# A graph network on one core: feed-forward products in groups of two node blocks, with all up products of a pair in one slot and both down products in the next

## The chip, the cores and the metric

The kernel runs on one core of one Trainium2 chip. The metric is device time in microseconds of one launch, smaller is better. The engines are named as in the profile: PE is TensorE (matmuls, with PEld its weight loads), DVE is VectorE, ACT is ScalarE, POOL is GpSimd and SP is SyncE. L12 is line 12 of the kernel.

## What is computed

A two-layer graph network on 10,000 nodes of 512 features and 160,000 edges that are sorted by target node. All data is fp32. Cut to what matters:

```python
# layer 0
h  = relu(layernorm(x))
ha = h @ rel_W[0..3] + rel_b              # four products per node
agg = segment_sum(ha[src, edge_type], dst) / max(deg, 1)
x1 = layer_norm(h + h @ self_W + self_b + agg, ln1_w, ln1_b)
f  = gelu(x1 @ W1 + b1) @ W2 + b2         # W1: 512 x 1024, W2: 1024 x 512
x  = x + layer_norm(x1 + f, ln2_w, ln2_b)
# layer 1: two SAGE layers on relu(layernorm(x))
h  = relu(layernorm(x))
for W_self, W_neigh, b in (...):
    h = relu(h @ W_self + segment_mean(h[src], dst) @ W_neigh + b)
x  = x + h
```

The change touches only the line that computes `f`, the feed-forward part of layer 0, and what is queued around it.

## The kernel before

The nodes are cut into 79 blocks of 128 (the last, number 78, has 16 nodes and is taken first). The program has three stages. Stage 1 (0 to 1611 us of the profiled execution) normalizes x and makes the five products of each block; beside it the edge lists are prepared. Stage 2 (1611 to 3616 us) does, for each block, the gather and sum of layer 0, both layer norms and the feed-forward part, and writes `xn`, the new x, and `h1`, the input of layer 1. The rest (3616 to 7341 us) is two SAGE layers over the same blocks. Only stage 2 is changed. The order of the instructions on each engine is that of the code, written out by hand; tiles come from pools with a given number of buffers, and an instruction that writes a buffer waits until the buffer's last readers are done.

**Gather and sums.** For a block, `gather` (L649) issues indirect DMAs on POOL, each bringing 128 rows of 2 KB into a row buffer. There is a ring of 28 such buffers (`RING`, L640). Each block has 5 "others", whose rows are summed over edges by one-hot matmuls, and 11 "mine" gathers, which are added on DVE (`add`, L688). Each 4th block adds a gather for a "tail" that is shared by 4 blocks, each 16th one that is shared by 16; tails have two buffers of their own. POOL issues in the order tails, others, mine. `sums` (L674) makes 7 matmuls on PE into a PSUM tile `pa`: first the two tails, then the others.

**The loop over blocks** (L903 to L932) is written as one slot for each block b. A slot holds, in this order: the load of `xs` for the block after next (SP, 512 KB for each pair of blocks); the one-hot tile of block b+1 (DVE); `second`, which adds the finished down products of the slot before to `rest` and takes their statistics (DVE); the adds of block b (11 on DVE), one scaling and statistics; then one part of the queued products on PE, but for its last call; then `finish` (a Sqrt on ACT over all statistics of the slot) and `scaled`; then the last call of the part; and last `begin` for block b+1, which is its gather on POOL and its sums on PE.

`scaled` (L848) applies norms on ACT: the first norm of block b, then the last norm of the blocks whose down products were two slots back (`h1`, stored by SP), then the second norm of those of the slot before. DVE then makes `rest` (what is added to the feed-forward result, 11 buffers) and the new `xr`, and SP stores `xn`.

**Groups.** Blocks are taken in groups of 4 (`plan`, L880): block 78 alone, then 19 groups of 4, then one of 2. A `Group` holds `x1T`, the transposed normalized block columns (two buffers, 512 columns wide), and `hid`, the hidden layer, transposed, 8 tiles of 128 x 512 (one buffer). `turn` makes 4 PE transposes and 4 ACT copies for one block; it is called in the middle of the slot after the block's own. `up(f)` makes 4 matmuls with up to 512 columns into `ph` (two PSUM buffers) and one Gelu on ACT into `hid`. `down(b)` loads `xr` (SP, for each pair of blocks) and makes 8 matmuls into `po` (two PSUM buffers). An fp32 matmul is two records in the trace.

`parts` (L791) cuts a group into four parts: ups 0 to 3, ups 4 to 7, the downs of its first two blocks, the downs of its last two. The parts of a group are put in the queue in the first slot of the next group, after that slot has taken its part; so they are taken one per slot from the slot after. Over a quad of slots, ups fall on the blocks with b%4 = 1 and 2 and downs on those with b%4 = 3 and 0. After the last block a closing loop (L935) takes what is left, one part in each pass, without gathers.

`Sqrt` and `Gelu` are in different activation tables; each change between them is a table load on ACT (L778, L821).

Of the kernel before, what the change touches and what calls it, by code (L numbers as in the profile page):

```python
# [8 lines left out]
F32 = mybir.dt.float32  # L9
# [7 lines left out]
P = 128  # L17
# [4 lines left out]
def kernel(  # L22
# [34 lines left out]
    N, D = x.shape  # L57
# [3 lines left out]
    KC = D // P  # L61
    FC = F // P
# [69 lines left out]
    def rows_of(t, g):  # L132

        b, nb, r = g
        return t[b * P:b * P + nb * r, :].rearrange("(c p) d -> p c d", p=r)
# [500 lines left out]
    def aligned(ctxa):  # L636
# [4 lines left out]
        rest = list(range(full))  # L641
        blocks = ([full] if N % P else []) + rest

        def height(b):
            return min(P, N - b * P)
# [49 lines left out]
        with ExitStack() as s:  # L695
            wp = s.enter_context(tc.tile_pool(name="wp2", bufs=1))
            gp = s.enter_context(tc.tile_pool(name="gp", bufs=1))
            sp = s.enter_context(tc.tile_pool(name="sp", bufs=3))
            psT = s.enter_context(tc.tile_pool(name="psT2", bufs=2, space=PSUM))
            psH = s.enter_context(tc.tile_pool(name="psH", bufs=2, space=PSUM))  # L700
# [8 lines left out]
            def pair(t, b, n, name, bufs):  # L709

                return (gp.tile([P, 2, D], F32, name=name, bufs=bufs)[:height(b), :n],
                        rows_of(t, (b, n, height(b))))
# [10 lines left out]
            def load_res(b, n):  # L723
                v, at = pair(xr_d, b, n, "xr", 3)
                nc.sync.dma_start(v, at)
                for c in range(n):
                    xrs[b + c] = v[:, c, :]
                xrs[b, n] = v
# [22 lines left out]
            class Group:  # L751


                def __init__(self, bs):
                    self.bs, self.r = bs, height(bs[0])
                    self.xT = gp.tile([P, KC, 4 * P], F32, name="x1T", bufs=2)
                    self.hid = None

                def turn(self, b, v):
# [10 lines left out]
                def up(self, f):  # L770
                    n = len(self.bs) * self.r
                    if self.hid is None:
                        self.hid = gp.tile([P, FC, 4 * P], F32, name="hid")
                    ph = psH.tile([P, 4 * P], F32, name="ph")
                    for k in range(KC):
                        nc.tensor.matmul(ph[:, :n], w1s[:, k, f * P:(f + 1) * P],  # L776
                                         self.xT[:, k, :n], start=(k == 0), stop=(k == KC - 1))
                    nc.scalar.activation(self.hid[:, f, :n], ph[:, :n], AF.Gelu,  # L778
                                         bias=b1s[:, f:f + 1], scale=1.0)

                def down(self, b):
                    c, r = self.bs.index(b), self.r
                    if c % 2 == 0:
                        load_res(b, min(2, len(self.bs) - c))
                    po = psO.tile([P, D], F32, name="po")
                    for f in range(FC):
                        nc.tensor.matmul(po[:r], self.hid[:, f, c * r:(c + 1) * r], w2s[:, f, :],  # L787
                                         start=(f == 0), stop=(f == FC - 1))
                    return b, po

                def parts(self):  # L791

                    ups = [lambda f=f: self.up(f) for f in range(FC)]
                    downs = [lambda b=b: self.down(b) for b in self.bs]
                    return [ups[:FC // 2], ups[FC // 2:]] + [downs[i:i + 2]
                                                             for i in range(0, len(downs), 2)]

            COLS = 8

# [32 lines left out]
            rests = {}  # L832
# [15 lines left out]
            def scaled(got, first):  # L848

                nonlocal third, now  # L850
                if first:
                    b, c = first
                    r, v = height(b), nodes[b]
                    now.apply(v[:r], v[:r], c, r, AF.Identity)
                if third:
                    h1, at = pair(h1_d, third[0][0], len(third), "h1", 2)
                    for k, (b, c) in enumerate(third):
                        now.apply(h1[:, k, :], xrs.pop(b), c, height(b), AF.Relu)
                    nc.sync.dma_start(at, h1)
                third = []  # L860
                for b, v, c in got:
                    r = height(b)
                    now.apply(v[:r], v[:r], c, r, AF.Identity)
                if first:
                    b, c = first
                    r, v = height(b), nodes[b]
                    rests[b] = gp.tile([P, D], F32, name="rest", bufs=11)
                    nc.vector.tensor_tensor(rests[b][:r], v[:r], ln1w[:r], op=OP.mult)
                    nc.vector.tensor_tensor(rests[b][:r], rests[b][:r], lnb2[:r], op=OP.add)
                now = Scales()  # L870
                for b, v, c in got:
                    r = height(b)
                    nc.vector.tensor_tensor(v[:r], v[:r], ln2w[:r], op=OP.mult)
                    nc.vector.tensor_tensor(xrs[b], xrs[b], v[:r], op=OP.add)
                    third.append((b, now.stats(xrs[b], r)))
                if got:
                    b, n = got[0][0], len(got)
                    nc.sync.dma_start(rows_of(xn_d, (b, n, height(b))), xrs.pop((b, n)))

            plan = [[b] for b in blocks[:len(blocks) - len(rest)]]  # L880
            plan += [rest[:-2][i:i + 4] for i in range(0, len(rest) - 2, 4)] + [rest[-2:]]
            queue = []
            turning = None
            held = begin(blocks[0], hots(blocks[0]), table)
# [18 lines left out]
            i = 0  # L903
            grp = None
            for bs in plan:
                for b in bs:
                    r = height(b)
                    if b == bs[0]:
                        before, grp = grp, Group(bs)
                    if i + 2 < len(blocks):  # L910
                        load(blocks[i + 2])
                    if i + 1 < len(blocks):
                        hot = hots(blocks[i + 1])
                    got = second()
                    pa, mine = held
                    add(b, pa, mine)
                    v = nodes[b]
                    nc.vector.scalar_tensor_tensor(v[:r], pa[:r], rdeg[:r, b:b + 1], v[:r],
                                                   op0=OP.mult, op1=OP.add)
                    first = (b, now.stats(v[:r], r))  # L920
                    part = products(queue.pop(0) if queue else [], turning)
                    next(part)
                    now.finish()
                    scaled(got, first)
                    next(part, None)
                    if i + 1 < len(blocks):
                        held = begin(blocks[i + 1], hot, table)

                    if b == bs[0] and before:
                        queue += before.parts()  # L930
                    turning = lambda g=grp, b=b, v=v: g.turn(b, v)
                    i += 1  # L932
            turning()
            queue += grp.parts()
            while queue or fed or third:  # L935
                got = second()
                part = products(queue.pop(0) if queue else [], None)
                next(part)
                now.finish()
                scaled(got, None)  # L940
                next(part, None)
# [6 lines left out]
        for step, (h_d, ws, wn, bs) in enumerate(((h1_d, ws1, wn1, bs1), (h2_d, ws2, wn2, bs2))):  # L948
            with ExitStack() as s:
# [54 lines left out]
                for i, b in enumerate(blocks):  # L1004
                    r = height(b)
                    q, c = place[b]
# [295 lines left out]
    with tc.If(go > 0) as cmp:  # L1302
        with ExitStack() as ctxa:
            with tc.manual_schedule():
                aligned(ctxa)
# [31 lines left out]
```

## Time and profile before

| | |
|---|---|
| three runs | 7339.11, 7335.75, 7313.08 us; median 7335.75 |
| profiled execution | 7342.91 us, of which the span of its instructions is 7341.1 |
| granted PE clock, mean | 0.881 |
| PE busy, whole span | 5665.5 us (77%) |
| DVE, POOL, ACT busy | 3658.8, 3792.5, 1016.3 us |
| stage 2, 1611 to 3616 us | PE 1700.0, DVE 1233.8, POOL 1248.4, ACT 583.1 us busy |
| DMA in stage 2 | 210 GB/s, the 16 DMA engines busy 69% |

How to read the lines below. A line of the timeline gives start and length in us, the engine, the line of the kernel, the operation, the tile written and the tiles read, shapes and how many equal instructions in a row it stands for; in brackets is the idle time of the engine just before, and what ended it. "issue" is a wait that the profile doesn't explain, "remote" one that ended with a signal whose sender it doesn't know. A view of stretches gives the busy time of each engine in a window, with the number of its instructions, then the granted PE clock as a share of full speed, the share of the DMA engines and GB/s.

### The profile page before, as it was taken

What the parts mean: (1) busy time and instruction counts of PE and PEld (TensorE: products, weight loads), DVE (VectorE), ACT (ScalarE), POOL (GpSimd) and SP (SyncE); (2) the same over time, 40 slices, a digit from 0 to 9 for tenths busy, and PEclk for the clock granted to TensorE, in tenths of its full rate; (3) what the DMA queues carried; (4) which work ended last, traced back from release to release, by engine and by line L of the source; (5) the groups of instructions that cost most, each with busy time, mean ns of one, the idle gap of its engine ahead of it and who ended that gap; (6) DMA issues with size and microseconds to landing.
All of it is one profiled execution on the core that took longest, in us unless ns stands there. A gap on an engine that the chain in (4) does not pass through costs nothing.

```text
span 7341.1 us, 49909 instructions
## 1 busy us (share of the span) xinstructions
PE 5665.5 (77%) x14251; PEld 2553.8 (35%) x14251; DVE 3658.8 (50%) x7297; ACT 1016.3 (14%) x1667; POOL 3792.5 (52%) x3927
## 2 busy tenths in 40 slices
PE   6999999986889889899766666766665666666666
PEld 3444444432334334344323332332322333332232
DVE  5347777424666666666334434443333444443444
ACT  1000000002232233233201100110100000000000
POOL 0000000016666666666266666666656666666665
PEclk9999999997999999999878888888887888888888
DMA  3222222236767777777366666666666777777775
GB/s 141 109 97 98 93 104 92 85 135 194 211 205 224 224 221 225 220 227 225 129 198 206 206 209 204 208 204 206 203 196 208 220 216 216 219 217 214 220 219 169
DMA packets 456992, 1361.46 MB, mean 185 GB/s; under 512 B 71746, under 2 KB 71746, under 8 KB 446578
## 3 DMA queue, kind: packets, MB, share of 16 engines
q0 software_dynamic: 308768, 1008.91, 46.5%
q1 hardware_dynamic: 134034, 262.10, 10.1%
q10 hardware_dynamic: 13904, 87.17, 3.0%
q8 instruction: 114, 1.87, 0.1%
q14 instruction: 172, 1.41, 0.1%
HBM read 1150.89 MB, written 207.01 MB: 185 GB/s over the span
## 4 chain that ended last, share of the span: by engine, by line
PE 39%; issue 20%; another core or an unknown queue 17%; ACT 3%; DVE 3%; DMA 1%; POOL 1%; ACTq 0%; POOLq 0%; DVEq 0%; SPq 0%
PE pa L680 11%; PE ph L776 6%; PE pm L613 6%; PE po L787 6%; PE po L984 4%; PE po L1018 4%; DVE pa L692 2%; PE pT L167 1%; POOL rows L653 1%; ACT hTb L168 1%; ACT mTb L168 1%; ACT mb L1014 0%; PE pT L764 0%; ACT hid L778 0%
## 5 line engine op out<-in xcount | busy, mean ns | idle before, releaser
L692 DVE TENSOR_TENSOR pa<-pa,rows 128x512 f32<-128x512 f32 x2574 | 1798.5, 699 | 1002.9 <-issue 689.3
L653 POOL DMA_INDIRECT rows<-h_d,row x1716 | 1663.6, 969 | 929.1 <-issue 428.5
L984 PE MATMUL po<-wns,mTb 128*128 128x512 f32 (+1 forms) x1264 | 704.5, 709 | 587.5 <-issue 310.2
L680 PE MATMUL pa<-rows,hot 128*128 128x512 f32 (+1 forms) x2358 | 1080.7, 605 | 46.1 <-issue 20.6
L653 POOL DMA_INDIRECT rows<-hall_d,row x858 | 849.8, 990 | 504.4 <-issue 193.7
L613 PE MATMUL pm<-wrel,hT 128*128 128x512 f32 (+1 forms) x2528 | 1098.1, 592 | 0.0
L1018 PE MATMUL po<-wss,hTb 128*128 128x512 f32 (+1 forms) x1264 | 700.6, 706 | 475.6 <-ACT hTb L168 387.3
L653 POOL DMA_INDIRECT rows<-h_d,orow x786 | 754.1, 959 | 400.1 <-issue 220.7
L776 PE MATMUL ph<-x1T,w1s 128*128 128x512 f32 (+2 forms) x1344 | 606.1, 605 | 158.9 <-ACT hid L778 111.4
L613 PEld LDWEIGHTS pm<-wrel,hT 128*128 128x128 f32 (+1 forms) x2528 | 477.0, 189 | 605.8 <-issue 595.3
L680 PEld LDWEIGHTS pa<-rows,hot 128*128 128x128 f32 (+1 forms) x2358 | 454.2, 193 | 641.9 <-issue 603.7
L984 PEld LDWEIGHTS po<-wns,mTb 128*128 128x128 f32 (+1 forms) x1264 | 280.8, 228 | 995.9 <-issue 691.6
L653 POOL DMA_INDIRECT rows<-hall_d,orow x393 | 373.1, 949 | 434.8 <-SPq L1333 308.5
L787 PE MATMUL po<-w2s,hid 128*128 128x512 f32 (+1 forms) x1264 | 561.4, 596 | 23.2 <-issue 20.8
L1018 PEld LDWEIGHTS po<-wss,hTb 128*128 128x128 f32 (+1 forms) x1264 | 273.7, 228 | 846.3 <-ACT hTb L168 440.4
L680 PE MATMUL pa<-tail,hot 128*128 128x512 f32 x936 | 457.7, 607 | 53.3 <-issue 49.2
L990 DVE TENSOR_TENSOR po<-po,bss 128x512 f32<-128x512 f32 (+1 forms) x79 | 55.0, 696 | 811.3 <-remote 702.7
L487 POOL DMA_INDIRECT win<-rec_d,at x79 | 74.8, 947 | 727.9 <-issue 637.1
L776 PEld LDWEIGHTS ph<-x1T,w1s 128*128 128x128 f32 x1344 | 263.8, 204 | 470.7 <-issue 332.1
L616 DVE TENSOR_TENSOR ha<-pm,brel 128x512 f32<-128x512 f32 (+1 forms) x316 | 216.4, 687 | 405.1 <-PE pm L613 405.1
L994 DVE TENSOR_TENSOR ob<-po,bss 128x512 f32<-128x512 f32 (+1 forms) x79 | 54.4, 688 | 597.4 <-remote 268.8
L787 PEld LDWEIGHTS po<-w2s,hid 128*128 128x128 f32 (+1 forms) x1264 | 236.2, 190 | 312.5 <-issue 308.0
(233 smaller groups left out, 4171.5 us busy)
## 6 DMA issues: line engine op xcount, KB each, us to landing
hall_d<-ha ACTq DMA_DIRECT2D x78, 1024.0 KB
hb<-h_d SPq DMA_DIRECT2D x38, 1024.0 KB
rows<-h_d,row POOLq DMA_INDIRECT x1716
xs<-xs_d SPq DMA_DIRECT2D x39, 512.0 KB
xr<-xr_d SPq DMA_DIRECT2D x39, 512.0 KB
xn_d<-xr SPq DMA_DIRECT2D x39, 512.0 KB
h_d<-h SPq DMA_DIRECT2D x39, 512.0 KB
xg<-in_x_dram SPq DMA_DIRECT2D x19, 1024.0 KB
```

The costliest lines, as they stand in the source:

```text
L167: nc.tensor.transpose(p[:, k, :r], rows[:, k * P:(k + 1) * P], ident[:r, :r])
L168: nc.scalar.copy(dest, p[:, :, :r])
L487: nc.gpsimd.indirect_dma_start(out=win[:, c, :], out_offset=None, in_=rec_d, in_offset=bass.IndirectOffsetOnAxis(ap=at[:, c:c + 1], axis=0))
L613: nc.tensor.matmul(pm[:r], hT[:, k, :r], w[:, k, :], start=(k == 0), stop=(k == KC - 1))
L616: nc.vector.tensor_tensor(ha[:r, j - 1, :], pm[:r], brel[:r, (j - 1) * D:j * D], op=OP.add)
L653: nc.gpsimd.indirect_dma_start(out=t[:n], out_offset=None, in_=table, in_offset=bass.IndirectOffsetOnAxis(ap=idx, axis=0))
L680: nc.tensor.matmul(pa[:r], hot[:, t, :r], others[t], start=(t == order[0]), stop=(t == order[-1]))
L692: nc.vector.tensor_tensor(pa[:r], pa[:r], t[:r], op=OP.add)
L776: nc.tensor.matmul(ph[:, :n], w1s[:, k, f * P:(f + 1) * P], self.xT[:, k, :n], start=(k == 0), stop=(k == KC - 1))
L787: nc.tensor.matmul(po[:r], self.hid[:, f, c * r:(c + 1) * r], w2s[:, f, :], start=(f == 0), stop=(f == FC - 1))
L984: nc.tensor.matmul(po[:r], mT[:, k, :r], wns[:, k, :], start=False, stop=(k == KC - 1))
L1018: nc.tensor.matmul(po[:r], hT[:, k, :r], wss[:, k, :], start=(k == 0), stop=False)
```

## The change

Groups have two blocks in place of four. A group has two parts: all eight ups (32 matmuls with 256 columns in place of 512, and 8 Gelus of 256 columns), and both downs. Over the loop, the ups of a pair now fall on blocks with odd b and the downs on those with even b. `x1T`, `hid` and `ph` have half as many columns; `load_res` is called once for each group; `rest` has 8 buffers in place of 11. The calls in a part stand around `finish` and `scaled` as before: with 8 ups, seven come before them and one after, and `turn` is called after the fourth; with 2 downs, one comes before and one after. Counted over the program, Gelus go from 168 to 320, and the table loads from 63 of each table to 80 of each. The matmuls of the downs, the gathers and the DVE adds are the same in number, and so are SP's loads and stores; the order of SP's list is another, with one of `xn`, `xs`, `xr` and `h1` for each pair.

```diff
@@ class Group
-                    self.xT = gp.tile([P, KC, 4 * P], F32, name="x1T", bufs=2)
+                    self.xT = gp.tile([P, KC, 2 * P], F32, name="x1T", bufs=2)
@@ def up(self, f)
-                        self.hid = gp.tile([P, FC, 4 * P], F32, name="hid")
-                    ph = psH.tile([P, 4 * P], F32, name="ph")
+                        self.hid = gp.tile([P, FC, 2 * P], F32, name="hid")
+                    ph = psH.tile([P, 2 * P], F32, name="ph")
@@ def down(self, b)
-                    if c % 2 == 0:
-                        load_res(b, min(2, len(self.bs) - c))
+                    if c == 0:
+                        load_res(b, len(self.bs))
@@ def parts(self)
-                    return [ups[:FC // 2], ups[FC // 2:]] + [downs[i:i + 2]
-                                                             for i in range(0, len(downs), 2)]
+                    return [ups, downs]
@@ def scaled(got, first)
-                    rests[b] = gp.tile([P, D], F32, name="rest", bufs=11)
+                    rests[b] = gp.tile([P, D], F32, name="rest", bufs=8)
@@ plan
-            plan += [rest[:-2][i:i + 4] for i in range(0, len(rest) - 2, 4)] + [rest[-2:]]
+            plan += [rest[i:i + 2] for i in range(0, len(rest), 2)]
```

## The prediction, as recorded before the result

> **What bounds the kernel now.** I read the page's list of engines, then the change's own stretch (stage 2, 1611 to 3616 us), then its waits, then the timelines of PE, ACT, POOL and SP inside single slots. "Slot" means one pass of the loop over blocks: products (one part of a queued group), then the sums of the next block. Busy time by stretch:
>
> ```profile
> core 0: us, PE busy (x) PEld busy (x) DVE busy (x) ACT busy (x) POOL busy (x), PEclk, DMA share, GB/s
> 1650.00:3502.00 1852.00, 1588.75 (x3747) 701.61 (x3747) 1165.44 (x1930) 534.68 (x859) 1220.13 (x1249) 0.92 0.72 217
> 3502.00:3616.00 114.00, 94.58 (x246) 47.85 (x244) 52.26 (x107) 47.02 (x70) 0.00 (x0) 0.92 0.16 56
> ```
>
> PE is busy 86% of the main stretch, ACT 29%. An undisturbed slot is all PE:
>
> ```profile
> 2561.91 7.03 PE L776 MATMUL ph<-x1T,w1s 128*128 128x512 f32 x16
> 2568.78 0.60 PE L764 MATMUL pT<-ident,xs 128*128 128x128 f32 x4
> 2569.22 7.03 PE L776 MATMUL ph<-x1T,w1s 128*128 128x512 f32 x16
> 2576.08 1.88 PE L680 MATMUL pa<-tail,hot 128*128 128x512 f32 x4
> 2577.80 4.46 PE L680 MATMUL pa<-rows,hot 128*128 128x512 f32 x10
> 2582.09 3.60 PE L776 MATMUL ph<-x1T,w1s 128*128 128x512 f32 x8
> ```
>
> From start to start, sums are 6.01 us, half the products 6.87, the transposes 0.44, the other half 6.87: 20.2 us. Taking every slot by the start of its first L680 matmul, 30 of the 68 slots from 1859 to 3502 us last 20.2 us, within 0.2; the mean of the 68 is 24.2. So stage 2 loses 4 us per slot, and the forecast is about where those lie. POOL is close behind: an issue takes 0.95 and a gap of 0.30, 1.25 us, times 16.3 gathers of a block is 20.4 us, and its pauses for the 28 ring buffers add more:
>
> ```profile
> 2560.42 0.94 POOL L653 DMA_INDIRECT rows<-hall_d,row  x1 [2.96 <-PE pa L680]
> 2583.57 1.12 POOL L653 DMA_INDIRECT rows<-hall_d,row  x1 [3.45 <-PE ph L776]
> 2608.31 0.94 POOL L653 DMA_INDIRECT rows<-hall_d,row  x1 [2.58 <-PE po L787]
> ```
>
> So POOL's cycle is some 23.5 us, and neither engine can be sped up alone. The largest losses are four slots of 41.8, 39.2, 45.7 and 39.2 us (at 1858.8, 1987.9, 2154.0 and 2928.4), all with ups. Inside the third, ACT and then PE:
>
> ```profile
> 2180.59 0.69 ACT L778 ACTIVATE hid<-ph,b1s 128x512 f32<-128x512 f32 x1 [18.13 <-issue]
> 2192.52 0.69 ACT L778 ACTIVATE hid<-ph,b1s 128x512 f32<-128x512 f32 x1 [11.24 <-remote]
> ```
>
> ```profile
> 2160.18 7.13 PE L776 MATMUL ph<-x1T,w1s 128*128 128x512 f32 x16
> 2181.33 5.75 PE L776 MATMUL ph<-x1T,w1s 128*128 128x512 f32 x8 [13.58 <-ACT hid L778]
> 2193.26 6.61 PE L776 MATMUL ph<-x1T,w1s 128*128 128x512 f32 x8 [6.17 <-ACT hid L778]
> ```
>
> The first ph was complete near 2164, its gelu began at 2180.59, with ACT idle and the table loaded. PE had two ph buffers, filled both, and stood for 13.6 and 6.2 us. In the slot at 2555.9 the same gelu began at 2565.55, at once. Comparing the end of each ph with the start of its gelu over the stage, the lag is 0.04 us in most cases within 8 us of a POOL pause, and 3.7 to 17 us once POOL has issued for more than 14 us without one. I read this as PE's signals arriving late while gathers run without a break. The trace shows the delay, not its cause.
>
> **What the Trainium skill says.** "TensorE: Matmul & The Clock Gate", Back-to-back issue gap: the gap goes with the free size, plus 2.5 ns. The trace agrees: 128x512 records are 0.43 us apart, the 128x256 ones at the stage's end 0.215 ("3569.68, x16 in 3.62 us"), weight loads hidden. "Perfetto Trace Analysis", Summary: the profiler window per engine type: for TensorE the end is estimated, and the semaphore's propagation is outside the record. The trace agrees: 16 us lie there above. Same page, Optimizing Scalar/DVE Operations: if ACT is not saturated but causes bubbles elsewhere, splitting instructions may complete work sooner. This speaks for the change; no row of before tests it at 256 columns beside gathers. "DMA: Bandwidth & Descriptors", Queues, rings and completion order: each engine alternates between its queues by packets, so a burst on SP's queue slows the gathers; SP issues four 512 KB transfers from 2505.18 to 2507.17, and the core's DMA engines are 99% busy from 2506 to 2522.
>
> **The change, part by part.**
>
> Matmuls. Ups per pair: 8 x 4 with 256 columns, at 2 records of 0.215 us, 13.7 us; before, 4 x 4 at 2 x 0.43, also 13.7. Downs unchanged. A slot's PE work stays 20.2 us, the total too: 0.
>
> ACT. Gelus go from 152 of 0.69 to 304 of 0.47 (the 256-column row at the end), +38 us; table loads for Gelu and for Sqrt, 63 each to 80 each, are 34 more at 1.28, +44 us. ACT has 1300 us idle in the main stretch: 0 on the path by itself. A load delays one gelu, priced with the round trip below. If that cover went, all 82 us would show.
>
> DVE, POOL. The same adds and gathers. Buffers: a rest lives 6 blocks with 8 buffers, as it lived about 9 with 11; x1T has two groups of buffers, hid one, read before its next write in PE's own order. No new wait: 0.
>
> SP. Per pair now xn, xs, xr and h1 leave in separate slots, where before a quad's D1 let off four at once, xr and xs having stood behind a store of h1 that waited for ACT (496 us in 20 waits of SP's queue). After the burst quoted above PE crawled through the next sums (2520.6 to 2536) and POOL paused 5.26 us. Moving the burst may give up to 6 us per quad, 18 x 6 = 108; it may also give nothing, as the crawl also follows from late signals alone. I take 0 and keep the gain for a rival.
>
> Tail. After the last block PE has no gathers beside it. Now it drains six part-slots there: U2, D1, D2 (13.7 each), then the last pair's U1, U2 (6.9 each) and D (13.7) = 68.6 us. After: D, U, D = 41.2. The 27.5 us move into early slots that had no products; the early ones wait for gathers (1610.9 to 1650: PE 16.7 of 39), so there they cost nothing, if block 78's slot does not get worse (now 59.9 us; all eight of its ups now share it). Gain 27.5, between 0 and 33 (the tail's 3.88 and 4.08 us waits included).
>
> The wait that is added. A U slot now makes eight round trips PE, ACT, PE, with two ph buffers each filled in 1.72 us in place of 3.43; so a signal may be 1.7 us late, not 3.4, before PE stands. Behind PE's ups stand the transposes, the rest of the ups, and the next block's sums, and behind those sums stand POOL's ring and DVE's adds. And U slots move: now ups fall on blocks with b%4 = 1 and 2, downs on 3 and 0; after, ups on each odd b, downs on each even. In the pass with b%4 = 3 POOL issues the gathers of a block with tails, which lie in buffers of their own, and I find its pause missing there in most quads: it runs some 40 us without a break (up to 2531.65, then 5.26 us). Now only downs lie there, which need nothing back from ACT; PE runs on and merely crawls. After, eight ups lie there. Bounds: at the least nothing (or a gain, as under SP); at the most, every such slot as long as the four above.
>
> Price: quads (four slots) that hold a starved slot last 102.4, 106.3, 106.2 and 108.9, mean 105.9; the 13 others average 93.8. One starved slot costs 12 us net, for a late PE lets POOL refill. There are 18 quads' worth, 4 starved now. I take two in three afterwards, 12: 8 x 12 = +96. Sum: 96 - 27.5 = +68.5. On the profiled execution (7342.9: span 7341.1 and 1.8 around it) 7411.4; that execution lies 7.2 above the median of 7335.75, so 7404.
>
> **The rivals.**
>
> Every quad starves: 14 x 12 = +168 - 27.5: about 7476. For: half the tolerance, twice the trips. Against: the present ups starve in four slots of 34 only.
>
> The other side, faster. One mechanism: U and D alternating keeps POOL pausing each slot, so no gelu is late, and the burst is gone: the four starved slots go, -48, and the tail, -27.5: 7260; with some of the burst's 108, lower. For: the gelu behind f5 falls due some 11 us after a pause, where about half the lags are still short. Against: lags above 14 us are always long, and the b%4 = 3 pause is missing. It decides at whether POOL pauses in that pass.
>
> Even: three more starved quads, +36 against -27.5: 7344.
>
> The change does what it says; ups and downs are cut in pairs in the text of the loop, and the order is fixed by that text.
>
> **How the numbers follow.** Chances: forecast 0.42, all starve 0.16, even 0.20, faster 0.22. 0.5%, or 37 us, is about what a measurement of this kernel can tell from no change: slower above 7372 has 0.58, same 0.20, faster 0.22. The likeliest sign's own range is 7375 to 7490. The range 7255 to 7490 leaves half of the faster case (0.11) and about half of the worst (0.08) outside.
>
> **What would show it.** Right: in after, slots with b%4 = 3 near 40 us with PE's ph waiting on ACT hid L778 well above its 111 us; tail after the last gather near 85 us, not 114; slots without stalls still 20.2. Wrong: a mean slot under 23 us and ph waits below 111 (then alternation helped), or L776's 256-column records further apart than 0.215 beside gathers (then the bound is PE). An execution whose early slots (to 1900 us) hold the difference would mean that block 78's eight ups decide.

## The result, and the profile after

The kernel after took 7540.45 us (median; 7529.55 to 7575.69) against 7330.53 for the kernel before beside it (7313.08 to 7339.11): 1.03 times the time of before, 95% interval 1.0266 to 1.0334. The forecast was 7404, slower; the range ended at 7490. The profiled execution of after took 7575.69, that of before 7342.91, 232.8 less.

The same stretch of stage 2, from the sums of the first blocks to the last gather (engines' busy time, then PE clock, DMA share, GB/s), is longer by 238 us, with the same work in it:

```profile
core 0: us, PE busy (x) PEld busy (x) DVE busy (x) ACT busy (x) POOL busy (x), PEclk, DMA share, GB/s
1650.00:3740.00 2090.00, 1590.61 (x4868) 947.60 (x4869) 1148.20 (x1914) 615.70 (x1034) 1202.96 (x1229) 0.87 0.61 190
```

PE and POOL are about as busy, in us, as in the 1852 us of before; there is just more idle time. PE's own waits in this stretch, in all, times, longest:

```profile
PE ph L776 <- issue: 292.6, 34, 24.1
PE ph L776 <- ACT hid L778: 206.2, 29, 30.1
PE pa L680 <- DMA rows<-hall_d,orow: 12.2, 1, 12.2
```

Before, the first two came to 39.5 and 107.3. Now 499 us of PE's idle time lie ahead of ups, nothing ahead of downs. A slot is counted as in the prediction, from the sums of a block to those of the next; a U slot runs the ups of a pair, a D slot its downs. D slots take 20.2 us, again and again; of the last 34 U slots, 31 take 32 to 48 us. Averaged over these 68 slots, U slots with b%4 = 1 take 34.0 us, those with b%4 = 3 take 36.2, D slots 20.2 and 20.2. One U slot (PE, ACT, POOL):

```profile
2345.94 1.88 PE L680 MATMUL pa<-tail,hot 128*128 128x512 f32 x4
2347.66 4.46 PE L680 MATMUL pa<-rows,hot 128*128 128x512 f32 x10
2351.95 7.07 PE L776 MATMUL ph<-x1T,w1s 128*128 128x256 f32 x32
2358.86 0.60 PE L764 MATMUL pT<-ident,xs 128*128 128x128 f32 x4
2359.29 3.86 PE L776 MATMUL ph<-x1T,w1s 128*128 128x256 f32 x16
2375.19 5.79 PE L776 MATMUL ph<-x1T,w1s 128*128 128x256 f32 x16 [12.03 <-ACT hid L778]
2380.81 1.88 PE L680 MATMUL pa<-tail,hot 128*128 128x512 f32 x4
```

```profile
2357.33 0.47 ACT L778 ACTIVATE hid<-ph,b1s 128x256 f32<-128x256 f32 x1 [1.25 <-issue]
2360.63 0.47 ACT L778 ACTIVATE hid<-ph,b1s 128x256 f32<-128x256 f32 x1 [2.83 <-PE ph L776]
2364.85 1.50 ACT L766 ACTIVATE x1T<-pT,ln1bc,ln1wc 128x128 f32<-128x128 f32 x4 [3.74 <-remote]
2374.66 0.84 ACT L778 ACTIVATE hid<-ph,b1s 128x256 f32<-128x256 f32 x2 [8.31 <-remote]
```

```profile
2352.06 0.94 POOL L653 DMA_INDIRECT rows<-hall_d,row  x1 [2.22 <-PE pa L680]
...
2370.81 0.95 POOL L653 DMA_INDIRECT rows<-hall_d,row  x1 [0.31 <-issue]
2383.82 1.39 POOL L653 DMA_INDIRECT rows<-hall_d,row  x1 [12.07 <-PE pa L680]
```

The first three Gelus are prompt, the fourth comes 1.6 us late, the copies after it 5.4 us after the transposes' end, and the fifth Gelu 13.5 us after its ph's end (2361.2), 2.9 us after POOL had issued the last gather that it could. The slot's length adds up: sums 6.0, then 19.7 us in which POOL issues 16 gathers (2352.06 to 2371.75), 2.9 until the signals come, 6.15 for the last ups: 34.8, and 34.87 is measured.

"Late" means late after the end that the profile gives for PE's matmuls. These ends are estimated, as the prediction says; whether the product or its signal is late, the trace can't tell.

In this slot PE's granted clock is halved as well, for 13.6 us (columns as in the first view):

```profile
2365.80:2379.40 13.60, 4.21 (x10) 3.41 (x11) 0.00 (x0) 1.78 (x5) 4.73 (x5) 0.50 0.42 127
```

That is not what starts the stall: the fourth Gelu was late at 2360.63 and PE stood from 2363.15. In 32 of the 34 U slots some Gelu or copy comes over 4 us late; in 31 of these the clock is halved in the slot, each time from 3 to 15 us after the first of its late signals had become 0.5 us late. The halved clock costs something afterwards, as the last ups take 5.79 us for 16 records in place of 3.6.

Where the 233 us lie: the start of stage 2 takes 49 us more (the sums of block 5 begin at 1798.0, not 1749.2), the 72 slots after it 240 more (1992.9 for 1752.5), the stretch from the last sums to the SAGE layers 40 less (88.1 for 127.7), the rest 17 less.

### The profile page after: what moved, and what is told of

It reads as the page before. It is cut to its first block, busy times and chain, and to the rows that moved or that the text cites. A ratio compares the mean times of both kernels' runs of the same rounds, so it can differ in the third digit from the quotient of the medians.

```text
span 7573.7 us, 52464 instructions
## 1 busy us (share of the span) xinstructions
PE 5662.2 (75%) x15467; PEld 2813.7 (37%) x15467; DVE 3655.4 (48%) x7295; ACT 1099.7 (15%) x1852; POOL 3796.2 (50%) x3927
## 4 chain that ended last, share of the span: by engine, by line
PE 39%; issue 19%; another core or an unknown queue 19%; ACT 3%; DVE 3%; DMA 1%; POOL 1%; ACTq 0%; POOLq 0%; DVEq 0%; SPq 0%
PE pa L680 10%; PE ph L776 8%; PE po L787 6%; PE pm L613 5%; PE po L983 4%; PE po L1017 4%; DVE pa L692 2%; PE pT L167 1%; DMA rows<-h_d,row 1%; POOL rows L653 1%; ACT hTb L168 1%; ACT x1T L766 1%; ACT mb L1013 0%; ACT mTb L168 0%
## 5 line engine op out<-in xcount | busy, mean ns | idle before, releaser
L680 PE MATMUL pa<-rows,hot 128*128 128x512 f32 (+1 forms) x2358 | 1061.0, 597 | 24.7 <-DMA rows<-hall_d,orow 13.2
L983 PE MATMUL po<-wns,mTb 128*128 128x512 f32 (+1 forms) x1264 | 681.6, 690 | 488.9 <-ACT mTb L168 290.6
L776 PE MATMUL ph<-x1T,w1s 128*128 128x256 f32 (+1 forms) x2560 | 662.7, 419 | 508.6 <-issue 301.8
L776 PEld LDWEIGHTS ph<-x1T,w1s 128*128 128x128 f32 x2560 | 533.1, 215 | 637.1 <-issue 336.0
L680 PE MATMUL pa<-tail,hot 128*128 128x512 f32 x936 | 442.3, 595 | 1.8 <-DVE mv L814 1.8
```

The source lines that it names most:

```text
L680: nc.tensor.matmul(pa[:r], hot[:, t, :r], others[t], start=(t == order[0]), stop=(t == order[-1]))
L776: nc.tensor.matmul(ph[:, :n], w1s[:, k, f * P:(f + 1) * P], self.xT[:, k, :n], start=(k == 0), stop=(k == KC - 1))
L983: nc.tensor.matmul(po[:r], mT[:, k, :r], wns[:, k, :], start=False, stop=(k == KC - 1))
```

## The experiments

The sets were run on different chips, and the chip turned out to matter: on three of them the kernel before takes some 6650 us, on the others 7323 to 7373. Each result is therefore given as a ratio to the kernel before in the same set. Lengths of slots in the first set are compared with the profiles of before and after above, which come from another chip (before: 7330.53 there, 7372.82 here).

Theory A: PE's signals to ACT come late once a certain number of PE instructions has followed the last pause of the gathers. Theory B: the slots starve because the two ph buffers hold half as much PE time as before (the room in ph). Theory A2, formed after the first set: the signals then wait for POOL to stop, and the ring says when.

**First set (before: 7372.82).** e1, the kernel before with narrow ups:

```diff
-                    for k in range(KC):
-                        nc.tensor.matmul(ph[:, :n], w1s[:, k, f * P:(f + 1) * P],
-                                         self.xT[:, k, :n], start=(k == 0), stop=(k == KC - 1))
+                    for c in range(0, n, 2 * P):
+                        m = min(n, c + 2 * P)
+                        for k in range(KC):
+                            nc.tensor.matmul(ph[:, c:m], w1s[:, k, f * P:(f + 1) * P],
+                                             self.xT[:, k, c:m], start=(k == 0),
+                                             stop=(k == KC - 1))
```

> The kernel before (quads), but each up matmul of 512 columns is issued as two of 256; Gelus, parts, buffers and order as before. Theory A (what counts is how many PE instructions follow the last pause of the gathers: signals to ACT come late after some 28 records): the two up slots of a quad, 64 records in place of 32, grow from 20 to 27 us to about 34, downs stay: some 7540 to 7600 us. Theory B (what counts is the room that ph gives, 1.72 us in place of 3.43, and the number of round trips): both are as in the kernel before, so 7335 within 40.

Measured 7460.87, ratio 1.0106 (1.006 to 1.0152), between the two. First up slots of a quad went from 25.8 to 34.5 us in the mean, second ones from 23.6 to 24.2, and the slot of the last two downs from 25.7 to 21.3. Only the ups' matmuls and their weight loads were doubled in number; ph's room and the Gelus are as before. So theory B alone doesn't explain it, and the first up slots starve as theory A says; its second half, that both do, fails. In the timeline of PE the second comes right behind a stall of 23 us, in which POOL too had to stop for 17.5, which may be what spares it.

```profile
3004.47 7.07 PE L778 MATMUL ph<-x1T,w1s 128*128 128x256 f32 x32
3011.38 0.64 PE L764 MATMUL pT<-ident,xs 128*128 128x128 f32 x3
3013.82 0.27 PE L764 MATMUL pT<-ident,xs 128*128 128x128 f32 x1 [1.80 <-issue]
3037.10 9.85 PE L778 MATMUL ph<-x1T,w1s 128*128 128x256 f32 x32 [23.01 <-ACT hid L781]
3046.78 1.88 PE L680 MATMUL pa<-tail,hot 128*128 128x512 f32 x4
```

e2, the kernel after with four ph buffers, two in one tile:

```diff
-                    ph = psH.tile([P, 2 * P], F32, name="ph")
+                    if f % 2 == 0:
+                        self.ph = psH.tile([P, 2, 2 * P], F32, name="ph")
+                    ph = self.ph[:, f % 2, :]
```

> The kernel after, with four ph buffers of 256 columns (two to a bank) in place of two. Theory B: the stall of 12 us in each slot of ups goes, since the first four Gelus are prompt: 7250 to 7330 us. Theory A: PE runs past the ups, but the signals stay late until the gathers pause, so that the downs of the next slot wait for hid, or PE crawls: part of the stall comes back there, 7380 to 7540.

Measured 7714.54, ratio 1.0445 (1.0384 to 1.0507), worse than both theories said. The edit is at fault: a product that goes into one half of a tile waits for the Gelu of the other half (0.56 us with "<-ACT hid L780" or "<-issue", ahead of each pair's second half in the slot at 3201.4). It gave less room, not more, and tells nothing of theory B but that a wait added here costs: U slots took 37.5 and 38.6.

e3, the kernel after with six of a block's eleven "mine" gathers in stage 2 (the first ones are added twice, so this kernel leaves rows out and its sums are others):

```diff
-            return others, [rows(P, row[:, b, t:t + 1]) for t in range(own(b))]
+            mine = [rows(P, row[:, b, t:t + 1])
+                    for t in range(min(6, own(b)) if few else own(b))]
+            return others, (mine * 2)[:own(b)]
```

> The kernel after, in which stage 2 leaves out five of the eleven mine gathers of a block (the first rows are added twice in their place); PE, ACT and DVE work unchanged. If the lateness comes from the unbroken stream of gathers (A): POOL is at 14 us per block, pauses over 5 us in each slot, the Gelus are prompt and slots of ups fall from 36 to 20 to 22 us: 6900 to 7000 us. If it comes from ACT's own chain (table loads, Sqrt, number of Gelus): slots of ups stay at 30 or more, above 7350.

Measured 7145.52, ratio 0.9675 (0.9619 to 0.9731). U slots fell to 26.4 (b%4 = 1) and 20.4 (b%4 = 3), with PE's, DVE's and ACT's work unchanged. So the products and Gelus fit into 20.4 us, and ACT's table loads and Sqrt, which are all still there, don't make the stall by themselves; the stream of gathers is needed for it. The tails say so too: behind the last sums, with no gathers left in stage 2, none of 18 signals is late in before or in after. The forecast of e3 was 150 to 250 us too low; that one U slot in two still loses 6 explains some 100 of it.

e4, pairs with four ups and one down of the pair before in each slot (two hid buffers; xr and h1 by blocks):

```diff
-                    return [ups, downs]
+                    out = [ups[:FC // 2] + owed[:1], ups[FC // 2:] + owed[1:]]
+                    owed[:] = [lambda b=b: self.down(b) for b in self.bs]
+                    return out
```

> Pairs as in the kernel after, but each slot takes four ups of a pair and then one down of the pair before (hid in two buffers, xr and h1 moved block by block). The fourth Gelu of a slot is followed by a down that needs nothing from this slot, so PE stands for no late signal. Theory A: the stalls of both kernels go, slots fall to POOL's cycle of 22.5 to 24: 7220 to 7330 us. Rival: the time is set by POOL's ring and the crawl of PE, and late signals just move: 7400 or more.

Measured 7576.05, ratio 1.0266 (1.0208 to 1.0323). 50 of 68 slots took 20 to 27.2 us, but 18 took over 30, all but one of them 40 to 46. There even an early Gelu of a slot is late: in the slot at 3244.7 the first starts at 3261.06, 8.4 us after ACT's table was loaded, and PE stands 6.80 and 11.73 us ahead of the third and fourth ups. A likely reading, not shown, is that POOL doesn't stop while no slot has to wait, and the lateness is carried from slot to slot. Placing work that needs no signal behind the ups saved nothing here: theory A's forecast failed, its rival's (7400 or more) came true.

**Second set (before: 6655.18).** e5 and e6, `RING = 22` in place of 28, in after and in before; e7, in after, a small memset on POOL behind each gather of stage 2; e8, after with three ph buffers:

```diff
+                if paced:
+                    nc.gpsimd.memset(gat.tile([P, 128], F32, name="pace", bufs=1), 0.0)
```

```diff
-            psT = s.enter_context(tc.tile_pool(name="psT2", bufs=2, space=PSUM))
-            psH = s.enter_context(tc.tile_pool(name="psH", bufs=2, space=PSUM))
+            psT = s.enter_context(tc.tile_pool(name="psT2", bufs=1, space=PSUM))
+            psH = s.enter_context(tc.tile_pool(name="psH", bufs=3, space=PSUM))
```

> The kernel after with 22 row buffers in place of 28 (in stage 2 and in the SAGE layers). Theory A2: once PE's signals are late, they come only when the gathers stop, and these stop when the ring is used up, so a slot of ups ends 6 x 1.25 = 7.5 us earlier: 34 to about 27 us, 38 slots, stage 2 shorter by 200 to 290 us. Rival: a smaller ring only blocks POOL earlier, and stage 2 gets longer. The SAGE layers have the same ring and may move either way by 100 us.

> The kernel before with 22 row buffers in place of 28. Theory A2: few of its slots starve, and each starved or crawling slot ends up to 7.5 us earlier: stage 2 shorter by 20 to 100 us, so 7230 to 7320 on the scale of 7330 if the SAGE layers stay. Rival: POOL is already near its limit, its pauses get longer, stage 2 longer by 50 or more.

> The kernel after with a memset of 128 x 128 on POOL behind each gather of stage 2, which makes the stream of gathers thinner by some 0.2 to 0.4 us per gather and changes nothing else. If it is the density of the gathers that holds back PE's signals: no late Gelus, slots of ups at POOL's new cycle of 23.5 to 26 us, stage 2 shorter by 100 to 300 us. If it is that POOL issues without a real pause, whatever the density: slots of ups as before or longer by POOL's added 3 to 6 us.

> The kernel after with three ph buffers (and one in place of two for the transposes). Its edit gives each of the eight round trips 3.4 us of room, as much as the kernel before had; the earlier try with four (two to a bank) did not, since PE waited for each Gelu of the same bank. Theory B (room): U slots fall from 34 to near 24 us, stage 2 shorter by 200 us or more. Theory A2: PE stands one product later, but for as long as POOL has ring buffers, so slots of ups stay at 32 to 36 us.

Measured: e5 6620.17, ratio 0.9948 (0.9928 to 0.9968); e6 6655.57, 1.0004 (0.9995 to 1.0012); e7 6753.54, 1.0148 (1.0128 to 1.0168); e8 6607.64, 0.9929 (0.9909 to 0.9949). None of the expectations came true, for the kernel before took 9% less time here and no slot starved: the longest of the last 68 slots took 27.5 us, in e6. This made the next question whether the kernel after is slower at all on such a chip.

**Third set (before: 6652.94).** The kernel after itself, and three of the kernels above.

> The kernel after, unchanged, beside the kernel before on the chip of this set. If the late signals of PE belong to the chip and not to the program: on a chip where the kernel before takes some 6650 us (no late Gelu), after is faster by the tail's 27 us and by what evenly spread SP transfers save, 6590 to 6625, ratio 0.990 to 0.996; on a chip where before takes some 7350 us, after is 7530 to 7600, ratio 1.03. If what made the chips differ is something else, the ratio is 1.03 on both.

> Three ph buffers once more. On a chip with late signals: theory B (room) U slots near 24 us, 7300; theory A2 (the stall lasts while POOL has ring buffers) slots of ups 32 to 36 us, 7500 to 7560. On a chip without: as the kernel after, within 10 us.

> 22 row buffers once more. On a chip with late signals, theory A2: slots of ups 27 us, stage 2 shorter than after's by 200 to 290 us; rival: no shorter. On a chip without: as the kernel after, within 20 us.

> The kernel before with each up matmul issued as two of 256 columns, once more. On a chip without late signals: theory A, the doubled PE instructions cost nothing there, 6655 within 15 us; rival (narrow matmuls cost PE time of their own beside gathers), 6700 or more. On a chip with late signals it is 1.01 of the kernel before again.

Measured: e9 6614.76, ratio 0.994 (0.9924 to 0.9957); e10 6616.56, 0.9944 (0.9924 to 0.9964); e11 6620.25, 0.9952 (0.9936 to 0.9967); e12 6651.96, 0.9993 (0.9984 to 1.0003). All four came out as expected for a chip without late signals. So the change is 3% slower on one chip and 0.6% faster on another. The main stretch, one U slot of PE and its ACT in e9:

```profile
1650.00:3220.00 1570.00, 1535.79 (x4915) 889.17 (x4914) 1150.48 (x1920) 620.99 (x1042) 1200.31 (x1213) 1.00 0.81 251
```

```profile
2409.52 7.07 PE L776 MATMUL ph<-x1T,w1s 128*128 128x256 f32 x32
2416.43 0.60 PE L764 MATMUL pT<-ident,xs 128*128 128x128 f32 x4
2416.86 7.07 PE L776 MATMUL ph<-x1T,w1s 128*128 128x256 f32 x32
2423.77 1.88 PE L680 MATMUL pa<-tail,hot 128*128 128x512 f32 x4
```

```profile
2416.63 0.48 ACT L778 ACTIVATE hid<-ph,b1s 128x256 f32<-128x256 f32 x1 [1.25 <-PE ph L776]
2417.06 1.51 ACT L766 ACTIVATE x1T<-pT,ln1bc,ln1wc 128x128 f32<-128x128 f32 x4
2418.79 0.47 ACT L778 ACTIVATE hid<-ph,b1s 128x256 f32<-128x256 f32 x1 [0.22 <-PE ph L776]
```

PE is busy 98% and POOL issues without a pause, at 251 GB/s, more than the 190 in the profile of after. A signal from PE to ACT is counted where a ph or the four transposes of a block are complete; it is late by the time from there, or from ACT's last instruction if that ends later, to the Gelu or copy. Of the 380 signals in stage 2 up to the last sums not one is over 0.04 us late in e9; in the profile of after 117 of 380 are over 0.5 us late, the longest 31 us, in that of before 68 of 228. The narrow matmuls of e12 cost nothing where no signal is late.

The clock is an obvious rival here, 1.00 in this stretch and 0.87 in after. But of the 117 late signals of after only 2 belong to products that end while the clock is halved, and of the 36 signals whose products end there 34 are on time. So in after the halved clock follows the stalls and doesn't bring them.

**Later sets.** These were meant for chips with late signals; e13 to e15 ran on one without (before: 6648.37), e16 and e17 on one with them (7323.38), e18 on another with them (7366.01).

> 22 row buffers in the kernel after, third set; aimed at a chip with late signals (before near 7350). Theory A2 (the stall lasts until POOL has used up the ring): slots of ups 27 us in place of 36, stage 2 shorter than after's by 200 to 290 us. Rival: slots of ups stay near 34 or the downs' slots grow. On a chip without late signals, 6620 again, and nothing is told apart.

> Three ph buffers in the kernel after, third set, aimed at a chip with late signals. Theory B (room of ph): slots of ups near 24 us. Theory A2: 32 to 36. On a chip without late signals, 6610 again.

> A memset of 128 x 128 on POOL behind each gather of stage 2 in the kernel after, aimed at a chip with late signals. There, if the density of the stream holds back the signals: slots of ups 22 to 26 us, stage 2 shorter than after's by 250 us or more. If the thinner stream holds them back as well: slots of ups 34 or more. On a chip without late signals it costs POOL's added time, 6750 again.

> 22 row buffers in the kernel after, for a chip with late signals (before near 7350). Theory A2: slots of ups 27 us in place of 36, stage 2 shorter than after's by 200 to 290 us. Rival: they stay near 34 or the downs' slots grow. On a chip without late signals 6615 again.

> Four ups and one down in each slot once more. On a chip without late signals PE never waited for a Gelu in the kernel after either, so mixing has nothing to save: after's 6615 within 15, or up to 20 more for the longer closing loop. On a chip with late signals 7570 again.

> The memset of 128 x 128 behind each gather of stage 2 in the kernel after, for a chip with late signals (before near 7350). If the density of the stream holds the signals back, slots of ups fall from 34 to 22 to 28 us and the ratio to before falls from 1.03 to 1.00 or below. If any stream without a pause does: the 16 gathers of a block take longer and slots of ups are 38 us or more, ratio 1.05 or more. On a chip without late signals 6750 again, ratio 1.015.

Measured: e13 6613.98, ratio 0.9941 (0.9919 to 0.9964); e14 6615.47, 0.9948 (0.9926 to 0.9971); e15 6750.05, 1.0151 (1.0121 to 1.018), all as expected for such a chip. e16 7534.83, 1.029 (1.0227 to 1.0353): U slots took 34.3 and 36.6 us, as with 28 buffers, so theory A2's forecast fails. POOL's timeline shows why:

```profile
2917.04 0.94 POOL L653 DMA_INDIRECT rows<-hall_d,row  x1 [2.55 <-PE pa L680]
...
2935.76 0.95 POOL L653 DMA_INDIRECT rows<-hall_d,row  x1 [0.30 <-issue]
2951.22 1.23 POOL L653 DMA_INDIRECT rows<-hall_d,row  x1 [14.51 <-PE pa L680]
```

Again 16 gathers from the resumption to the stop (2917.04 to 2936.7). The buffers that POOL waits for here are those which the sums on PE free, and the sums come once per block; a smaller ring shifts which row of the block meets the wait, not how many rows lie between two sums. So POOL stops one block after the last sums whatever the ring, and e16 doesn't test whether the signals wait for that stop. The trace of after speaks for it only in part: in the 32 U slots with a signal over 4 us late, the latest one comes 2.2 to 3.0 us after POOL's last gather in 13, as in the slot above, within 1.6 us of it in 10, and in 9 while POOL goes on issuing.

e17 7505.37, 1.025 (1.022 to 1.0281), as in e4. e18 7545.67, 1.0238 (1.0147 to 1.0329), between its two forecasts: the memset takes 0.22 us, but most of it fits into the gap between two gathers, which follow each other every 1.34 us in place of 1.25 (medians). U slots took 30.7 and 37.7 us, a little less and a little more than after's. A stream that is thinner by one part in fifteen holds the signals back nearly as much; a much thinner one was tried only in e3. More room in ph (theory B) was not tried on a chip with late signals: e8, e10 and e14 all met others. So the part that room has in the loss is open, and e1, with 88 us over its before, shows only that narrow matmuls are enough for some of it. No version beat both kernels on both kinds of chip.

## Why the prediction was wrong

**What was right.** Slots without a stall kept 20.2 us, and 256-column records stood 0.215 us apart beside gathers as well (32 in 7.07), half of the 0.43 for 512 columns, as priced; the 2.5 ns on top are too little to be seen in these figures. ACT took 83 us more over the program (1099.7 for 1016.3; 82 expected) and this cost nothing by itself. The place of the loss, PE standing ahead of ups for a late Gelu, and its sign were as described. SP's transfers, taken at 0: on a chip without late signals e12, which is the kernel before but for its narrow ups and as fast, can be set against e9. The slot of the last downs fell from 23.4 to 21.3 us, the other three went from 20.3, 20.3 and 20.5 to 21.1, 20.3 and 21.7, and the mean of the 68 is 21.10 in e12 and 21.12 in e9. Nothing gained, as priced. (Beside SP's burst the trace has the DMA engines 96% busy from 2506 to 2522 us, not 99%; no price rests on that.)

**The tail** was mis-sized by some 10: 27.5 expected, 40 and 36 measured (127.7 to 88.1; 127.3 in e12 to 91.3 in e9). On the chip of the result about half of the 12 us more are waits of PE in the tail of before, which the prediction had put into its upper end of 33; the rest are products that ran slower there. At the start the moved products were to cost nothing. Without late signals that is nearly so: e9 is 16 us behind e12 at the sums of block 5 (1727.5 and 1711.3), but 3 at those of block 9. The 49 us on the chip of the result have late signals in them: block 78's ups grew their slot, as feared, from 60 to 74 us, and in the slot of block 3, which took 52 us, a Gelu came 31 us late.

**The step that failed** is the price of the added wait. It let only the slots with b%4 = 3 starve, for 12 us net in two of three quads, +96. In nearly all quads both U slots starve (31 of 34 slots take over 30 us), so that 72 slots, or 18 quads, cost 240. Even the worst rival, with all 14 other quads, counted one starved slot in each and +168. The likely reason is the scale on which the lateness was read: in us since POOL's pause (mostly short within 8 us, about half short near 11, always long beyond 14), and so the ups behind a pause seemed safe. Take as a pause each gap of over 1 us between two gathers, take the signals that came when ACT stood idle, and call those late that come after 0.5 us. By time since the pause, before has 4 late of 22 at 6 to 8 us, 2 of 7 at 8 to 10 and 15 of 20 at 10 to 12; after has 15 of 40 at 4 to 6 and 46 of 46 at 6 to 8. By the number of PE's matmul records since the pause the two are much nearer: at 16 to 23, 7 of 26 and 4 of 31; at 24 to 31, 17 of 24 and 22 of 42; at 32 to 39, 12 of 13 and 39 of 45. Narrow matmuls make records twice as fast, so the fifth up of a U slot now falls into the late zone, and the pause that came in time for a slot of 32 records comes too late for one of 64. e1 is the trial of this, with the result above. That the count itself is the cause is not shown: each matmul record has a weight load beside it, beyond 48 records the two profiles part again (16 late of 19 and 13 of 39 at 48 to 63), and e18 has 3 late of 22 at 24 to 31.

**What a single profile couldn't tell.** Whether signals come late went with the chip that a set ran on: the same after is 1.03 of before on one and 0.994 on another, where the tail's 27.5 and no other term is near the 38 us measured. The faster rival had the right sign there, but by another way: it had the alternation of U and D take late signals away, and on that chip there were none. No chip was used in two of the sets e1 to e18, so whether it is the chip itself or something on it at that time is not shown. What differs between these chips is open; the traces show the late signals and no cause.

## What to carry to other kernels

When a profile shows signals that come late, count on which scale they do (time, instructions, bytes) before pricing a change that moves one of them: here the time scale said safe, and the count of PE's records, read from the same profile, would have said late. Splitting wide matmuls need not be free even if PE's own time is unchanged: alone it cost 1.1% on a chip with late signals (e1) and nothing on one without (e12). And a verdict of a few per cent that rests on such waits should be taken on more than one chip.

## What was not expected of the hardware

Two kinds of chip in these sets: with the same program, the kernel before takes 6646 to 6663 us on three chips and 7313 to 7419 on the others; granted PE clock over the whole span 0.936 and 0.867 for after. In stage 2 PE's signals to ACT stay within 0.04 us on the first kind with gathers at 251 GB/s, and come up to 31 us late on the second at 190. The second kind is slower in the SAGE layers as well, which the change doesn't touch: from their first sums to the end before takes 3712 us, e12 on the first kind 3282. There too signals come late on the second kind alone: of the 316 times that ACT copies four transposes, 127 are over 0.5 us late in before, none over 0.1 in e9 and e12.
